# One VectorE product of 2048 columns for two units of a selective scan, in place of two of 1024

## The chip, the cores and the metric

The kernel runs on one core of a Trainium2 chip. The metric is the device time of one execution in microseconds (us), as the median of several runs. Before the change it is 11,066.46 us (three runs, 11,062.12 to 11,069.53). Lower is better. The engines of a core are named as the profile names them: PE (TensorE, matrix products), DVE (VectorE), ACT (ScalarE), POOL (GpSimd) and SP (SyncE, whose queue issues the transfers here). PSUM is the memory that PE writes, eight banks of 512 fp32 columns on each of 128 partitions; the large on-chip memory is SBUF.

## The reference, cut to what matters

The input is eight images of 96 channels and 64 x 64 pixels. The first layer normalizes them, runs a VSS block (a state space block with a two-dimensional selective scan) and a convolutional block with channel attention; the second layer is a linear attention and a feed-forward net in low precision. Nearly all of the time goes into the selective scan:

```python
def selective_scan(xs, dts, A, Bs, Cs, Ds, dt_bias):
    delta = jax.nn.softplus(dts + dt_bias[None, :, :, None])
    ...
    def step(h, inp):
        u_t, d_t, b_t, c_t = inp
        dA = jnp.exp(d_t[..., None] * A)
        h = dA * h + (d_t * u_t)[..., None] * b_t[:, :, None, :]
        y = jnp.einsum('bkdn,bkn->bkd', h, c_t)
        return (h, y)
```

It runs over 4096 pixels, in 4 directions k, for 192 inner channels d with 16 states n each, for each image. For every (image, direction, channel, state) there is a recurrence h = dA * h + (delta * u) * B along the pixels, with B and C depending on direction, state and pixel but not on the channel. The output y is the sum over the 16 states of h * C.

## The kernel before, in words

**Tiling.** Images go in pairs p (four of them), directions k, chunks ci of 1024 pixels (CH), and three tiles T of 128 channels of a pair (192 channels of two images make 384 rows). A *job* is (p, k, ci, T), 192 jobs in all. A job has 16 *units* (j, q): j picks 32 of the tile's 128 channels, q picks 4 of the 16 states, so a unit is 32 x 4 = 128 rows on the partitions and 1024 pixels along the free dimension. Four units with the same j are a *group* g. There are 3072 units, and they are worked off two at a time: 1536 rounds.

**What a unit does.** `fetch` (L1290) loads delta of a group, each channel repeated for four states, into `dl`; `decay` (L1304) makes dA = exp(A * delta) on ACT into `da` (four buffers). `spread` (L1299) has PE copy delta * u of a group, each channel for four states, into the PSUM tile `pu` (1024 columns, two banks) with two matmuls; all four units of the group read it. `weights` (L1268) loads four rows of B (i = 0, tile `bm`) or of C (i = 1, tile `cm`), repeated 32 times over the partitions, 512 KB each; a tile serves all units with the same job triple, batch and q, so there are 512 loads of each kind. `bm` has four buffers, `cm` five.

**The round.** `scan(u)` (L1311) does two units. On DVE it makes the two products pu * B into the two PSUM tiles `pb0` and `pb1` (L1316, L1317), and then the two recurrences with `tensor_tensor_scan` (L1318 to L1324), which read `da` and `pb` and write `hc` (eight buffers); for the later chunks they start from the column `carry`. On POOL it saves the last column as the next `carry` and multiplies `hc` by C (L1326 to L1331). `total` (L1349) then has PE sum the states of a group in PSUM tile `yp`, 16 matmuls, and ACT copies the sum out. For directions 2 and 3 the scan runs backwards over the columns (step -1).

**The order.** All engines of this part are wrapped in `InOrder` (L254), which keeps each engine's instructions in the order of the Python program; this is why most records of the profile carry L266. The main loop (L1400 to L1446) goes through the rounds: it runs one step of the background work, then `scan(u)`, then issues the B loads for units u+4 and u+5 (L1432), the C loads for u+2 and u+3, the decays of u+2 and u+3, and after a group's second round the `spread` of the next group and the `total` of the one before. The background work (convolutions, projections, gates, normalizations of other image pairs) is handed out step by step by the class `Slots` (L283) and runs mainly on PE, ACT and POOL. Waits between engines are semaphores. So are waits of one engine's instruction for another one of the same engine, where the second reads or overwrites what the first wrote or read. An instruction carries one wait itself; further waits stand in separate semaphore instructions ahead of it in the engine's queue, which can hold two each.

**PSUM.** `yp` and `pg` take one bank each, `pu` two, `pb0` and `pb1` two each: eight.

After the loop a tail of some 340 us finishes the last pair (normalizations, attention, feed-forward); ahead of it phase_a prepares the first pair in some 215 us.

Of the kernel before, what the change touches and what calls it, by code (L numbers as in the profile page):

```python
# [9 lines left out]
F32 = mybir.dt.float32  # L10
# [17 lines left out]
CH = 1024  # L28
# [322 lines left out]
def phase_b(  # L351
# [8 lines left out]
    with ExitStack() as ctx:  # L360
# [57 lines left out]
        for i in range(2):  # L418

            t = cp.tile([C + 1, 512], F32, name=f"tn{i}")  # L420
# [3 lines left out]
        bcp = inner.enter_context(tc.tile_pool(name="b_bc", bufs=4))  # L424
# [3 lines left out]
        psc = inner.enter_context(tc.tile_pool(name="b_ps", bufs=1, space=PSUM))  # L428
# [5 lines left out]
        yps = psc.tile([128, 512], F32, name="yp")  # L434
        bank0 = psc.tile([128, 512], F32, name="pg")
        pu = psc.tile([128, CH], F32, name="pu")
        pbs = [psc.tile([128, CH], F32, name=f"pb{i}") for i in range(2)]
        pe = InOrder(tc, nc.tensor, mybir.EngineType.PE)
        ve = InOrder(tc, nc.vector, mybir.EngineType.DVE)
        se = InOrder(tc, nc.scalar, mybir.EngineType.Activation)  # L440
# [6 lines left out]
            for ci in range(NCH) for T in (0, 2, 1)  # L447
        ]
        units = [(job, j, q) for job in range(len(jobs)) for j in range(4) for q in range(4)]
        carries, bcs, dus, dls, sts, das, hcs, prevs, yet = ({} for _ in range(9))  # L450
        turned, resting, squeezed_at = set(), set(), set()

        def where(job):
            p, k, ci, T = jobs[job]
            c = NCH - 1 - ci if k >= 2 else ci
            return p, k, ci, c, T, slice(c * CH, c * CH + CH)

        def batch(u):
            job, j, q = units[u]
            T = jobs[job][3]  # L460
            return j // 2 if T == 2 else T
# [806 lines left out]
        def weights(u, i):  # L1268

            if u >= len(units):  # L1270
                return
            job, j, q = units[u]
            p, k, ci, c, T, at = where(job)
            b = batch(u)
            if (job // 3, b, q, i) in bcs:
                return
            t = bcp.tile([128, CH], F32, name=("bm", "cm")[i], bufs=(4, 5)[i])
            r0 = 32 * (k // 2) + 16 * i + 4 * q
            nc.sync.dma_start(
                t, xd_d[k % 2][2 * p + b][r0 : r0 + 4, at].unsqueeze(0).to_broadcast([32, 4, CH])  # L1280
            )
            bcs[job // 3, b, q, i] = t

# [27 lines left out]
        def scan(u):  # L1311

            job, j, q = units[u]
            p, k, ci, c, T, at = where(job)
            step, last = (-1, 0) if k >= 2 else (1, CH - 1)
            for i in range(2):  # L1316
                ve.tensor_mul(pbs[i], pu, bcs[job // 3, batch(u), q + i, 0])  # L1317
            for i in range(2):  # L1318
                t = hp.tile([128, CH], F32, name="hc")
                carry = carries[p, k][:, T, 4 * j + q + i : 4 * j + q + i + 1]  # L1320
                ve.tensor_tensor_scan(
                    t[:, ::step], das.pop(u + i)[:, ::step], (pbs[i])[:, ::step],
                    0.0 if ci == 0 else carry, ALU.mult, ALU.add,
                )  # L1324
                hcs[u + i] = t
            for i in range(2):  # L1326
                v = u + i
                carry = carries[p, k][:, T, 4 * j + q + i : 4 * j + q + i + 1]
                if ci < NCH - 1:
                    ge.tensor_copy(carry, hcs[v][:, last : last + 1])  # L1330
                ge.tensor_mul(hcs[v], hcs[v], bcs[job // 3, batch(u), q + i, 1])  # L1331
# [61 lines left out]
        for u in range(4):  # L1393
            weights(u, 0)
        for u in range(2):
            weights(u, 1)
# [3 lines left out]
        for u in range(0, n, 2):  # L1400
            g, q = divmod(u, 4)
            if q == 0:
                if g % 4 == 0:
                    job = g // 4 + 1
                    assert slots.first is None
                    p, k, ci, T = jobs[g // 4]
# [15 lines left out]
                    if job < len(jobs):  # L1422
                        p, k, ci, c, T, at = where(job)
# [4 lines left out]
            elif g + 2 < n // 4:  # L1428
                fetch(g + 2)
            slots.run()  # L1430
            scan(u)
            for v in range(u + 4, u + 6):  # L1432
                weights(v, 0)
# [35 lines left out]
        p = NP - 1  # L1469
# [336 lines left out]
def block(tc, a, out):  # L1806
    with tc.tile_pool(name="dram", bufs=1, space=DRAM) as dp:
# [29 lines left out]
        with tc.tile_pool(name="p_const", bufs=1) as pp:  # L1837
            phase_b(
                tc, a, pp, xi_d, xd_d, dl_d, ya_d, ys_d, y_d, zs_d, inp_d, x1_d, ua_d, u_d, g_d,
                cb_d, tn_d, out,  # L1840
            )
# [105 lines left out]
```

## Time and profile before

| | before |
|---|---|
| median of three runs | 11,066.46 us |
| lowest and highest | 11,062.12 and 11,069.53 us |
| span of the profiled execution, first to last instruction | 11,058.4 us |
| mean granted TensorE clock in it | 0.815 |
| DVE's first product of the loop starts | 214.6 us into the span |
| last scan starts | 10,721.3 us |
| products pb on DVE | 3072, 1197 / 1220 / 1251 ns (least, median, most) |
| scans with a carry | 2304, 2310 / 2335 / 2366 ns |
| scans without one | 768, 2254 / 2275 / 2307 ns |
| POOL product hc by cm | 3072, mean 2359 ns |
| ACT decay da | 3072, mean 1140 ns |
| PE spread into pu | 3072 matmuls, mean 944 ns |
| HBM traffic over the span | 165 GB/s |

The profile is one execution taken by the hardware profiler; its span leaves out what lies around the program, so it is put beside the median and not in its place. A group's line reads: line, engine, operation, tile written and tiles read, shapes, number; then the summed busy time and the mean of one; then the idle time of the engine just before them and what ended most of it. The profile counts an instruction from its start to its end, and neighbours on one engine can overlap, so lengths may add up to more than the time that passes. A timeline line reads: start in us, length of the merged group, engine, line, operation, tiles, shapes, number, and in brackets the idle time before it with its releaser, if over 0.15 us. Semaphore instructions are not shown there and not counted as busy.

### The profile page before, as it was taken

To read this page: it belongs to the slowest core of one execution; us is meant where nothing else is said; L and a number is where in the kernel's file an instruction comes from. 1 tells how busy PE (TensorE), PEld (TensorE's weight loads), DVE (VectorE), ACT (ScalarE), POOL (GpSimd) and SP (SyncE) were. 2 spreads that over 40 slices of the span, in tenths; PEclk is the share of its full clock that TensorE was granted. 3 is DMA by queue.
4 is the path that set the end of the run, shared out by engine and by line. 5 is a ranking of instruction groups with operands and counts; after the bars stand their busy time and mean duration, and the time that the engine had idled before them with its cause. 6 is when DMAs were issued, how large, how long until landed. Compare 5 with 4: busy or idle time off the path is not lost.

```text
span 11058.4 us, 128094 instructions
## 1 busy us (share of the span) xinstructions
PE 7887.2 (71%) x39468; PEld 3111.6 (28%) x39468; DVE 10525.7 (95%) x6651; ACT 6596.3 (60%) x9175; POOL 9028.7 (82%) x6649
## 2 busy tenths in 40 slices
PE   7755778655568887767777787776767776665778
PEld 3322333222223332223222332223322222222223
DVE  4999999999999999999999999999999999999974
ACT  2544765544567666556776656565776656665554
POOL 2788877787898888998888887899889888988860
PEclk8877888877788888878878888887878877777889
DMA  3445554454555555666545555566544555644551
GB/s 117 151 165 180 160 156 157 141 188 156 163 185 172 171 172 157 211 214 195 158 152 160 157 178 159 177 220 209 172 157 159 160 164 179 197 157 140 173 157 37
DMA packets 900188, 1834.20 MB, mean 166 GB/s; under 512 B 247965, under 2 KB 421214, under 8 KB 892462
## 3 DMA queue, kind: packets, MB, share of 16 engines
q1 hardware_dynamic: 899502, 1826.01, 52.8%
q8 instruction: 314, 5.14, 0.2%
q14 instruction: 372, 3.05, 0.1%
HBM read 1405.13 MB, written 420.42 MB: 165 GB/s over the span
## 4 chain that ended last, share of the span: by engine, by line
PE 32%; issue 29%; DVE 17%; POOL 11%; ACT 6%; DMA 4%; SPq 0%; DVEq 0%; POOLq 0%; ACTq 0%
PE pu L266 12%; PE yp L266 11%; DVE hc L266 11%; POOL hc L266 7%; PE pg L266 6%; DVE pb L266 5%; ACT u L266 2%; ACT da L266 2%; POOL u L266 2%; PE t L266 2%; PE ps L197 1%; DMA bm<-xd 1%; POOL turn L266 1%; POOL carry L266 1%; ACT L266 1%
## 5 line engine op out<-in xcount | busy, mean ns | idle before, releaser
L266 POOL TENSOR_TENSOR hc<-hc,cm 128x1024 f32<-128x1024 f32 x3072 | 7230.0, 2359 | 591.0 <-DVE hc L266 382.6
L266 DVE TENSOR_TENSOR_SCAN hc<-da,carry,pb 128x1024 f32<-128x1024 f32 x2304 | 5276.8, 2334 | 38.1 <-ACT da L266 31.5
L266 PE MATMUL pu<-du,c_sel 128*128 128x512 f32 x3072 | 2452.5, 944 | 2244.1 <-DVE pb L266 2239.6
L266 DVE TENSOR_TENSOR pb<-pu,bm 128x1024 f32<-128x1024 f32 x3072 | 3601.6, 1220 | 133.9 <-PE pu L266 105.9
L266 ACT ACTIVATE da<-dl,c_alog 128x1024 f32<-128x1024 f32 x3072 | 3352.8, 1140 | 91.4 <-DVE hc L266 73.8
L266 PEld LDWEIGHTS pu<-du,c_sel 128*128 128x128 f32 x3072 | 790.0, 281 | 3521.1 <-DVE pb L266 2784.8
L266 DVE TENSOR_TENSOR_SCAN hc<-da,pb 128x1024 f32<-128x1024 f32 x768 | 1713.1, 2275 | 38.9 <-ACT da L266 22.8
L266 ACT COPY y<-yp 128x256 f32<-128x256 f32 x768 | 284.4, 370 | 2348.9 <-PE yp L266 2198.4
L266 PE MATMUL yp<-hc,c_add 128*32 128x256 f32 x24576 | 1660.8, 416 | 22.6 <-ACT s L266 6.6
L266 PEld LDWEIGHTS yp<-hc,c_add 128*32 128x32 f32 x24576 | 768.6, 120 | 1200.1 <-issue 628.4
L266 POOL COPY carry<-hc 128x1 f32<-128x1 f32 x2304 | 422.5, 183 | 766.1 <-DVE hc L266 744.9
L266 ACT ACT_TABLE_LOAD x566 | 726.2, 1283 | 38.2 <-DMA cb<-zs 16.9
L266 ACT COPY u<-pg 128x512 f32<-128x512 f32 (+6 forms) x397 | 218.3, 550 | 712.3 <-PE pg L266 641.2
L266 POOL TENSOR_TENSOR u<-u,u 96x512 f32<-96x512 f32 (+1 forms) x426 | 537.5, 1269 | 105.9 <-ACT u L266 101.8
L266 POOL TENSOR_TENSOR du<-du,dls 128x1024 f32<-128x1024 f32 x192 | 452.7, 2358 | 91.5 <-ACT dls L266 91.1
L266 ACT COPY u<-yp 96x512 f32<-96x512 f32 (+6 forms) x347 | 188.0, 542 | 465.5 <-PE yp L266 404.5
L266 PE MATMUL pg<-ain,wmain 96*128 96x512 f32 x792 | 354.1, 599 | 0.0
L266 PE MATMUL pg<-ain,wmix 96*128 96x512 f32 x792 | 353.0, 598 | 0.0
L266 PE MATMUL yp<-prev,ident 128*128 128x256 f32 x768 | 321.9, 512 | 39.0 <-ACT u L266 27.4
L266 PEld LDWEIGHTS yp<-prev,ident 128*128 128x128 f32 x768 | 214.5, 283 | 381.8 <-issue 264.3
L266 PE MATMUL pg<-st,dtw 12*128 12x512 f32 x384 | 218.5, 649 | 49.4 <-ACT u L266 28.8
L266 PE MATMUL yp<-st,dtw 12*128 12x512 f32 x384 | 227.9, 674 | 18.3 <-ACT u L266 10.9
(340 smaller groups left out, 7030.2 us busy)
## 6 DMA issues: line engine op xcount, KB each, us to landing
dl<-dl SPq DMA_DIRECT2D x768, 512.0 KB
bm<-xd SPq DMA_DIRECT2D x512, 512.0 KB
cm<-xd SPq DMA_DIRECT2D x512, 512.0 KB
du<-xi SPq DMA_DIRECT2D x192, 512.0 KB
dl<-dls SPq DMA_DIRECT2D x192, 512.0 KB
ya<-y SPq DMA_DIRECT2D x384, 128.0 KB
prev<-ya SPq DMA_DIRECT2D x384, 128.0 KB
xi<-u SPq DMA_DIRECT2D x152, 256.0 KB
```

The source lines that it names most:

```text
L197: nc.tensor.matmul(bank[r, :].rearrange("p (h w) -> p h w", w=W), w[:, t if len(which) > 1 or w is wmix else 0, columns], pads[b][:, 8 * j ...
L266: op(*args, **kw)
```

## The change

The two PSUM tiles `pb0` and `pb1` become one tile `pb` of 2 x 1024 columns (the same four banks). The B loads of two units (q even and q odd) go into the two halves of one SBUF tile `bm` of 2 x 1024 columns, with two buffers in place of four of half the size; the tile is taken when the even half is loaded. In `scan`, one `tensor_mul` of 2 x 1024 columns replaces the two of 1024: `pu` is read twice through a dimension of stride 0, `bm` whole, and `pb` is written whole. The two scans read a half of `pb` each. C loads, scans, POOL, PE and ACT work and the loop stay as they are.

```diff
-        pbs = [psc.tile([128, CH], F32, name=f"pb{i}") for i in range(2)]
+        pb = psc.tile([128, 2, CH], F32, name="pb")
...
-            t = bcp.tile([128, CH], F32, name=("bm", "cm")[i], bufs=(4, 5)[i])
+            if i:
+                t = to = bcp.tile([128, CH], F32, name="cm", bufs=5)
+            else:
+                if q % 2 == 0:
+                    pairs[job // 3, b, q] = bcp.tile([128, 2, CH], F32, name="bm", bufs=2)
+                t = pairs[job // 3, b, q - q % 2]
+                to = t[:, q % 2, :]
             r0 = 32 * (k // 2) + 16 * i + 4 * q
             nc.sync.dma_start(
-                t, xd_d[k % 2][2 * p + b][r0 : r0 + 4, at].unsqueeze(0).to_broadcast([32, 4, CH])
+                to, xd_d[k % 2][2 * p + b][r0 : r0 + 4, at].unsqueeze(0).to_broadcast([32, 4, CH])
             )
             bcs[job // 3, b, q, i] = t
...
-            for i in range(2):
-                ve.tensor_mul(pbs[i], pu, bcs[job // 3, batch(u), q + i, 0])
+            ve.tensor_mul(
+                pb, pu.unsqueeze(1).to_broadcast([128, 2, CH]), bcs[job // 3, batch(u), q, 0]
+            )
             for i in range(2):
                 t = hp.tile([128, CH], F32, name="hc")
                 carry = carries[p, k][:, T, 4 * j + q + i : 4 * j + q + i + 1]
                 ve.tensor_tensor_scan(
-                    t[:, ::step], das.pop(u + i)[:, ::step], (pbs[i])[:, ::step],
+                    t[:, ::step], das.pop(u + i)[:, ::step], pb[:, i, ::step],
                     0.0 if ci == 0 else carry, ALU.mult, ALU.add,
                 )
                 hcs[u + i] = t
```

More of the change, by code (lines that the diff above doesn't have):

```diff
@@ L449, in phase_b @@
         units = [(job, j, q) for job in range(len(jobs)) for j in range(4) for q in range(4)]
-        carries, bcs, dus, dls, sts, das, hcs, prevs, yet = ({} for _ in range(9))
+        carries, bcs, pairs, dus, dls, sts, das, hcs, prevs, yet = ({} for _ in range(10))
         turned, resting, squeezed_at = set(), set(), set()
```

## The prediction

> **What bounds the kernel now.** I read the busy times first, then the slices, then VectorE's groups, then the timeline of a stretch in the middle.
>
> ```profile
> PE 7887.2 (71%) x39468; PEld 3111.6 (28%) x39468; DVE 10525.7 (95%) x6651; ACT 6596.3 (60%) x9175; POOL 9028.7 (82%) x6649
> ...
> DVE  4999999999999999999999999999999999999974
> ```
>
> VectorE (DVE) is busy for 95% of the span and at 90% or more in every slice but the first and the last two. POOL follows with 82%. So the time between about 215 us and 10,724 us, the scan loop, is VectorE's own stream of instructions, and what lengthens or shortens that stream moves the end by as much.
>
> ```profile
> L266 DVE TENSOR_TENSOR_SCAN hc<-da,carry,pb 128x1024 f32<-128x1024 f32 x2304 | 5276.8, 2334 | 38.1 <-ACT da L266 31.5
> ...
> L266 DVE TENSOR_TENSOR pb<-pu,bm 128x1024 f32<-128x1024 f32 x3072 | 3601.6, 1220 | 133.9 <-PE pu L266 105.9
> ```
>
> The loop is 1536 rounds of two products (pb) and two scans (hc). Other engines hold VectorE up very little: 134 us in front of products, 77 us in front of the two kinds of scans (38.1 here, 38.9 in the group without a carry), 211 us in all. The next view, a timeline of VectorE, tells what a round takes (start, length of the merged group, instructions in it):
>
> ```profile
> 5001.25 2.34 DVE L266 TENSOR_TENSOR pb<-pu,bm 128x1024 f32<-128x1024 f32 x2
> 5003.50 4.57 DVE L266 TENSOR_TENSOR_SCAN hc<-da,carry,pb 128x1024 f32<-128x1024 f32 x2
> 5007.99 2.34 DVE L266 TENSOR_TENSOR pb<-pu,bm 128x1024 f32<-128x1024 f32 x2
> ```
>
> Two products of 1.22 us make 2.34 us and not 2.44: neighbours overlap. The next group starts before the last ends: 5001.25 + 2.34 = 5003.59, against 5003.50. In the trace's instruction records the medians from start to start are product to product 1.115 us, product to scan 1.130, scan to scan 2.254, scan to product 2.238. A round is their sum, 6.737 us (5007.99 - 5001.25 = 6.74). Every instruction starts some 0.09 us before the one ahead has ended, so the recorded lengths overstate what an instruction costs. **This overlap is what the change puts at stake.**
>
> **Who waits for whom.** In the built program before, each product and scan waits for VectorE's own semaphore, but always for the instruction before the last one: order P0 P1 S0 S1, where S0 needs P0, S1 needs P1, the next P0 overwrites what S0 read, the next P1 what S1 read. One instruction always lies between, so that wait has long been met. In the program after, the order is P S0 S1. S0 needs P, the instruction directly ahead; the next P overwrites both halves of pb, so it waits for S1, directly ahead too. Only S1 keeps a free start. All 1536 S0 and nearly all P have such a wait.
>
> **What a wait for the instruction directly ahead costs.** The loop of before has none, but the tail after it has some 75, on VectorE too:
>
> ```profile
> 10778.22 1.54 DVE L266 SCALAR_TENSOR_TENSOR tn<-tn,c_on,cb 128x512 f32<-128x512 f32 x2 [2.17 <-ACT cb L266]
> ```
>
> Two instructions of 752 ns each in one buffer, the second reading the first: 1.54 us is 2 x 0.752 + 0.035. No overlap, and a gap of 34 to 36 ns from end to start; 48 casts behind a TENSOR_SCALAR show the same. That is the price where the waiting instruction itself carries the wait. Where an instruction has more waits than it can carry, the others stand in a separate semaphore instruction ahead of it, and this costs more:
>
> ```profile
> 10803.93 0.75 DVE L266 SCALAR_TENSOR_TENSOR w_dt.float<-t,c_vec,w_dt.float 96x512 f32<-96x512 f32 x1 [8.99 <-ACT w_dt.float L266]
> 10804.78 2.44 DVE L266 TENSOR_SCALAR up<-w_dt.float,c_vec 96x512 f32<-96x512 f32 x1
> ...
> 10809.96 0.75 DVE L266 SCALAR_TENSOR_TENSOR w_dt.float<-t,c_vec,w_dt.float 96x512 f32<-96x512 f32 x1 [1.49 <-ACT w_dt.float L266]
> 10810.74 0.48 DVE L266 TENSOR_SCALAR up<-w_dt.float,c_vec 96x512 f32<-96x512 f32 x1
> ```
>
> The first pair goes through such a semaphore instruction: 10804.78 - 10803.93 - 0.747 = 0.107 us of gap. The second pair waits directly: 10810.74 - 10809.96 - 0.747 = 0.036 us. A semaphore instruction with two waits is recorded at 50 ns instead of 21, so with the late wait listed first I take 0.107 + 0.029 = 0.136 us.
>
> **The sum for a round.**
> - The joint product: a product of 512 columns (tn) takes 684 ns, of 1024 columns 1220, so 536 ns for 512 columns, and 1220 + 2 x 536 = 2292 ns for 2048. [...]
> - P to S0: S0's wait for P stands in a semaphore instruction with two waits (P first, then ScalarE): 0.136. From P's start to S0's start 2.292 + 0.136 = 2.428, against 1.115 + 1.130 = 2.245 now: **+0.183**.
> - S0 to S1: free as before, 2.254: 0.
> - S1 to the next P: S1 takes 2.324. Half of the products (those behind no new pu) carry the wait themselves, 0.035; the other half, which also wait for PE's new pu, have it in a semaphore instruction, 0.107; mean 0.071. So 2.395 against 2.238: **+0.157**.
>
> Together +0.340 us a round, x 1536 = **+522 us**. The rounds without a carry (a quarter) have start to start times 60 ns shorter before and after; the difference is the same.
>
> Off this I take: S0 now starts on a drained engine, and a scan behind a scan is 16 ns shorter from start to start than one behind a product (2.238 against 2.254): -25 us. The same for the joint product (a product behind a scan is recorded at 1209, one behind a product at 1224; 11 ns below my 1220): -17 us. And some of the 211 us that VectorE now idles for others goes: a round is 5% longer for PE, ScalarE and the loads alike, and where VectorE waits for another engine its own gap is hidden. Bounds 0 and 100 us; I take 30, since 115 such stops of 0.1 to 0.2 us hidden are about 17 and the rest is catching up. Sum 522 - 25 - 17 - 30 = **+450 us**.
>
> **What lies beside it and costs nothing.** The B loads keep their place in SP's queue and their number (512); two buffers of two units hold what four of one did. The first load of a pair may now be issued only when the joint product is done, about 1.1 us later than now, and the joint product needs the second half 1.1 us earlier; the loads are issued two rounds (13 us) ahead. The view of pb shows how close this is now:
>
> ```profile
>   PE pu L266: 105.9, 45
>   ACT da L266: 54.3, 43
>   DMA bm<-xd: 25.3, 19
> ```
>
> Only 19 products waited for a load, 25 us in all. The cover is the two rounds, which grow by 0.68 us. If the cover were gone, each of the 256 first uses of a pair would lose up to 1.1 us, 282 us; I take 0. PE's spread into pu is released by the end of a round's last product and needed by the next round's first, two scans later; that window grows from 4.40 us (1.130 - 1.220 + 2.254 + 2.238) to 4.82 (0.136 + 2.254 + 2.324 + 0.107). PSUM stays at eight banks. POOL and ScalarE get the same work at a slower pace.
>
> [...] The row: dependent neighbours stand 0.035 to 0.107 us apart, free ones overlap by 0.09. [...]
>
> **The rivals.**
> - *The waits cost nothing (faster).* If S0 could start on P's tail as now, P to S0 would be 1.115 + 2 x 0.536 = 2.187 (free start), against 2.245: -0.058 x 1536 = -89 us, **10,977**. The change stops being slower where the two gaps, 0.207 us together in my sum, have become an overlap of 0.133 (0.207 - 0.340); none of the tail's dependent pairs starts before the one ahead has ended. 4%: 3% faster, 1% where gain and loss cancel.
> - *Only one of the two holds costs, or each only the direct 35 ns.* P to S0 alone: 0.183 x 1536 = +281; both at 35 ns: (2.327 - 2.245) + (2.359 - 2.238) = 0.203, +312. Less the same 72 us of relief: **about 11,290**. Against it: the built program has both waits, and in which place. 6%.
> - *The loads become late.* Forecast plus up to 282 us: **11,600 to 11,800**. Against it the 25 us above. 7%.
> - *The change isn't in the program.* The built program has 1536 products of 2048 columns instead of 3072 of 1024. 0%.
>
> **How the numbers follow.** The profiled execution spans 11,058.4 us; the median of three runs is 11,066.46, 8 us more, which I keep: 11,066 + 450 = **11,516**. Forecast 83%. Lower end: hold of 0.107 instead of 0.136 (-45) and 100 us of idle time back instead of 30 (-70): 11,400. Upper end: none of the 72 us of relief and some 20 us of late loads: 11,610. Measurement can tell about 0.2% (22 us) from no change. Faster 3%, same 1%, slower 96%.
>
> **What would show it.** After the change: 1536 products of about 2.28 us; start to start about 2.42 us from product to scan, scan to scan still 2.25, scan to product 2.36 or 2.43 in turn; VectorE's busy time falls, since the overlap is no longer counted twice, while the span grows. I am wrong if the scan's start overlaps the product's end, or if the waits for bm grow past 100 us.

## The result and the profile after

The changed kernel takes **11,511.7 us** (median of four runs, 11,505.08 to 11,519.01) against 11,067.99 for the kernel before beside it (four runs). The ratio is 1.040, with a 95% interval of 1.0387 to 1.0414: **slower by 4%**, 444 us. The forecast was 11,516 us. The profiled execution spans 11,514.0 us, 455.6 more than that of before. The 12 us between 444 and 455.6 are a matter of which execution was profiled: that of before spans 10 us less than the median of its kernel, that of after 2 us more.

The page of after, busy times, VectorE's row of slices, and its three large groups:

```profile
PE 7973.9 (69%) x39468; PEld 3138.2 (27%) x39468; DVE 10735.8 (93%) x5115; ACT 6605.7 (57%) x9175; POOL 9032.1 (78%) x6649
...
DVE  4999999999999999999999999999999999999974
...
L266 DVE TENSOR_TENSOR_SCAN hc<-da,carry,pb 128x1024 f32<-128x1024 f32 x2304 | 5281.5, 2334 | 168.5 <-ACT da L266 13.0
...
L266 DVE TENSOR_TENSOR pb<-pu,bm 128x2048 f32<-128x2048 f32 x1536 | 3532.2, 2300 | 200.3 <-PE pu L266 71.5
...
L266 DVE TENSOR_TENSOR_SCAN hc<-da,pb 128x1024 f32<-128x1024 f32 x768 | 1714.4, 2274 | 79.9 <-PE yp L266 14.2
```

VectorE still bounds the kernel: 90% or more in every slice but the first and the last two. It issues 1536 instructions fewer, and the joint product of 2300 ns is shorter than two of 1220. So by recorded lengths the change is a gain of 140 ns a round. The loss is in two places. VectorE's busy time rose by 210 us, because neighbours that overlapped no longer do. The rest stands in the last column: the idle time ahead of scans and products has gone from 211 us to 449 (168.5 + 200.3 + 79.9), and the releasers named explain only a part of it. In front of the carry scans, ACT's decay accounts for 13.0 of 168.5 us. The rest is spread over 1152 scans, the first of each round with a carry, as gaps too short to be listed. In the trace's records of the loop, gaps of up to 0.15 us add up to 299 us after and to 1 us before; longer ones fell from 189 us to 129. Idle time without a releaser, in many small equal pieces, is what a wait for the same engine's own previous instruction looks like here.

The timeline of after, VectorE (start, length of the merged group, number):

```profile
5299.24 4.59 DVE L266 TENSOR_TENSOR_SCAN hc<-da,carry,pb 128x1024 f32<-128x1024 f32 x2
5303.86 2.30 DVE L266 TENSOR_TENSOR pb<-pu,bm 128x2048 f32<-128x2048 f32 x1
5306.30 4.58 DVE L266 TENSOR_TENSOR_SCAN hc<-da,carry,pb 128x1024 f32<-128x1024 f32 x2
5310.98 2.30 DVE L266 TENSOR_TENSOR pb<-pu,bm 128x2048 f32<-128x2048 f32 x1
5313.41 4.58 DVE L266 TENSOR_TENSOR_SCAN hc<-da,carry,pb 128x1024 f32<-128x1024 f32 x2
```

Add start and length and compare with the next start. 5303.86 + 2.30 = 5306.16, and the scan starts at 5306.30: a gap of 0.13 us (0.14 with these rounded figures). 5306.30 + 4.58 = 5310.88, and the product starts at 5310.98: 0.10. 5299.24 + 4.59 = 5303.83, next start 5303.86: 0.03. Before, each of these sums lay *past* the next start by 0.09. Nothing is named as a releaser, because no other engine is late.

The views by tile, of after, show the waits for other engines in front of the joint product and its scans (us, times):

```profile
  PE pu L266: 71.5, 28
  ACT da L266: 25.8, 17
  DMA bm<-xd: 22.3, 9
```

All three are smaller than before (105.9, 54.3, 25.3): a slower VectorE gives everybody else more time. That holds for PE too, though its granted clock was 0.803 against 0.815 and its spread took 968 ns against 944. The loads, which now come in pairs, didn't become late.

### The profile page after: what moved, and what is told of

Same layout as the page of the kernel before. It is cut to its first block, busy times and chain, and to the rows that moved or that the text cites. A ratio compares the mean times of both kernels' runs of the same rounds, so it can differ in the third digit from the quotient of the medians.

```text
span 11514.0 us, 124663 instructions
## 1 busy us (share of the span) xinstructions
PE 7973.9 (69%) x39468; PEld 3138.2 (27%) x39468; DVE 10735.8 (93%) x5115; ACT 6605.7 (57%) x9175; POOL 9032.1 (78%) x6649
## 5 line engine op out<-in xcount | busy, mean ns | idle before, releaser
L266 DVE TENSOR_TENSOR_SCAN hc<-da,carry,pb 128x1024 f32<-128x1024 f32 x2304 | 5281.5, 2334 | 168.5 <-ACT da L266 13.0
L266 PE MATMUL pu<-du,c_sel 128*128 128x512 f32 x3072 | 2519.7, 968 | 2691.7 <-DVE pb L266 2687.2
L266 DVE TENSOR_TENSOR pb<-pu,bm 128x2048 f32<-128x2048 f32 x1536 | 3532.2, 2300 | 200.3 <-PE pu L266 71.5
L266 DVE TENSOR_TENSOR_SCAN hc<-da,pb 128x1024 f32<-128x1024 f32 x768 | 1714.4, 2274 | 79.9 <-PE yp L266 14.2
L266 ACT ACT_TABLE_LOAD x566 | 726.2, 1283 | 37.7 <-DMA cb<-zs 18.1
```

What stands on the lines that cost most here:

```text
L266: op(*args, **kw)
```

## The experiments

The question is which part of the change costs the 444 us. My theory: the two holds, that is, S0 and P now waiting for the instruction directly ahead of them on their own engine. Rivals: the joint tiles by themselves (four banks, paired loads), the instruction of 2048 columns by itself, and late loads. None of the runs leaves out work of the reference. Times of the kernel before beside them lie between 11,069 and 11,075 us. S to P and the like below are medians from start to start, in us, in rounds with a carry where nothing from another engine is late.

| run | time, us | ratio to before (95%) |
|---|---|---|
| joint tiles, two products | 11,777.4 | 1.0641 (1.0625 to 1.0656) |
| paired loads alone | 11,078.2 | 1.0007 (0.9998 to 1.0016) |
| product and scan in turn | 12,814.5 | 1.1578 (1.1561 to 1.1595) |
| in turn in half of the rounds | 11,415.1 | 1.0308 (1.0293 to 1.0322) |
| touch ahead | 11,739.8 | 1.0607 (1.0591 to 1.0623) |
| products in SBUF | 15,808.8 | 1.4283 (1.4259 to 1.4307) |
| places swapped | 11,095.9 | 1.0025 (1.0014 to 1.0035) |
| one hold gone | 11,299.4 | 1.0207 (1.0192 to 1.0223) |
| product a round ahead | 11,522.4 | 1.0410 (1.0394 to 1.0425) |
| the same, phase moved | 11,461.2 | 1.0348 (1.0334 to 1.0362) |
| sums and loads earlier | 12,074.3 | 1.0910 (1.0895 to 1.0925) |
| decays split | 12,276.3 | 1.1091 (1.1075 to 1.1106) |

**The joint tiles, with two products of 1024 columns** (from after):

```diff
-            ve.tensor_mul(
-                pb, pu.unsqueeze(1).to_broadcast([128, 2, CH]), bcs[job // 3, batch(u), q, 0]
-            )
+            for i in range(2):
+                ve.tensor_mul(pb[:, i, :], pu, bcs[job // 3, batch(u), q, 0][:, i, :])
```

> Both tiles joined as in the change (bm of two units, pb of two halves), but two products of 1024 columns again, each on its half. My theory: each wait is again for the instruction before the last one, so a round is 6.737 us and the time that of before, 11,066 us (11,040 to 11,095). Rival, the joined tiles cost the time (loads of a pair that must both have landed, buffers freed two units at a time): it stays near 11,510 us.

Measured 11,777.4: a miss, and the expectation was badly thought out. In the built program waits go by tile, not by half: P1 waits for P0 because both write pb, S0 waits for P1, the next P0 for S1. That is three holds in place of none. The timeline of this run:

```profile
5303.20 2.50 DVE L266 TENSOR_TENSOR pb<-pu,bm 128x1024 f32<-128x1024 f32 x2
5305.84 4.58 DVE L266 TENSOR_TENSOR_SCAN hc<-da,carry,pb 128x1024 f32<-128x1024 f32 x2
```

Two products take 2.50 instead of 2.34: P0 to P1 is 1.267 (a gap of 0.035) where it was 1.115, and P1 to S0 is 1.365 (a gap of 0.133) where it was 1.130. So the run says nothing about the tiles alone. It shows two other things: a hold costs the same with narrow products, and where the tile is joint anyway, the joint *instruction* is the better one, by 266 us (11,777.4 - 11,511.7).

**The paired loads alone** (from before: the joint `bm` tile, everything else as it was; its last changed line is):

```diff
-                ve.tensor_mul(pbs[i], pu, bcs[job // 3, batch(u), q + i, 0])
+                ve.tensor_mul(pbs[i], pu, bcs[job // 3, batch(u), q, 0][:, i, :])
```

> Only the B loads go into a joint tile of two units (two buffers), as in the change; pb stays two tiles and the products stay two of 1024 columns. Unlike in the run with both tiles joined, no instruction now waits for the one directly ahead. My theory: the time of before, 11,066 us (11,040 to 11,095). Rival, loads that must land in pairs and buffers freed in pairs cost part of the 445 us: over 11,150 us, with more waits of products for bm than the 25 us of before.

Measured 11,078.2, ratio 1.0007, and 27.9 us of waits for bm: no cost. Loads and the `bm` tile are out.

**Product and scan in turn** (from before; order P0 S0 P1 S1, so that each scan directly follows its product, and no instruction is wider):

```diff
                 ve.tensor_mul(pbs[i], pu, bcs[job // 3, batch(u), q + i, 0])
-            for i in range(2):
                 t = hp.tile([128, CH], F32, name="hc")
```

> The kernel before with another order on VectorE: product, scan, product, scan; no joint product and no joint tile. Each scan now reads what the instruction directly ahead wrote; no product overwrites what the instruction directly ahead read. My theory: two holds of 0.133 us and two lost overlaps, product to scan 1.220 + 0.133 = 1.353 us, scan to product 2.238 as before, a round 2 x (1.353 + 2.238) = 7.182 us, +0.445 x 1536 = +683 us, less up to 130 us of idle time that comes back: 11,620 to 11,750 us. Rival, the width of the joint instruction costs the time: 11,066 us, as the instructions are the same as before.

Measured 12,814.5: the undisturbed round is 2 x (1.339 + 2.264) = 7.206, as expected (a hold of 0.13 between product and scan, with narrow products in tiles of their own), but 1,000 us more came from somewhere else:

```profile
L266 DVE TENSOR_TENSOR pb<-pu,bm 128x1024 f32<-128x1024 f32 x3072 | 3723.9, 1212 | 889.0 <-PE pu L266 867.2
```

The group of products waits 867 us for PE's spread, and the two groups of scans wait another 262 us for PE's sums in yp. In this order the last product that reads pu stands one scan later, so PE has the time of one scan to fill pu again instead of two. That was still an argument until the next run.

**In turn only in rounds behind which pu is not refilled** (from before; P0 S0 P1 S1 for q = 0, P0 P1 S0 S1 for q = 2):

```diff
-                ve.tensor_mul(pbs[i], pu, bcs[job // 3, batch(u), q + i, 0])
-            for i in range(2):
+                if i == 0 or q == 0:
+                    ve.tensor_mul(pbs[i], pu, bcs[job // 3, batch(u), q + i, 0])
+                if i == 0 and q == 2:
+                    ve.tensor_mul(pbs[1], pu, bcs[job // 3, batch(u), q + 1, 0])
```

> The kernel before with the order product, scan, product, scan only in the first round of each group; in the second round, whose last product frees pu for PE, both products come first as before. This tells why the order in turn in every round cost 1745 us where I had expected 550 to 680. My theory: the surplus was PE, which there had one scan's time to refill pu and here has two again; so only the holds of half the rounds are left, 0.47 us x 768 = +360 us less up to 100 us of stalls that come back: 11,290 to 11,430 us, and products wait for pu some 100 us in place of 867. Rival, the order in turn costs its surplus in every round: half of 1745, about 11,940 us.

Measured 11,415.1. With pu's window left as it was, the waits for pu are 79.9 us instead of 867.2, and the loss is the holds': 768 x 0.469 (7.206 - 6.737) = 360 us by this, and some 341 found (11,415.1 less 11,415.1 / 1.0308). The gap of a held scan is the 0.133 us of the changed kernel here too, with narrow products and another order.

**Touch ahead** (from after; a copy of one column of da into the first scan's `hc` buffer ahead of the product, so that the waits for ACT and for the buffer are met there and S0 has only the wait for P):

```diff
+            ts = [hp.tile([128, CH], F32, name="hc") for i in range(2)]
+            ve.tensor_copy(ts[0][:, 0:1], das[u][:, 0:1])
...
-                t = hp.tile([128, CH], F32, name="hc")
+                t = ts[i]
```

> The changed kernel with one more VectorE instruction a round, ahead of the joint product: a copy of one column of da into the buffer that the first scan will write whole. It takes the first scan's waits for ScalarE, PE and POOL, so that the scan carries its wait for the product itself, without semaphore instructions ahead. My theory: product to scan falls from 2.432 to 2.335 us (gap 0.035 in place of 0.133), and the copy itself lies in the gap between the second scan and the product; scan to product about 2.36 in place of 2.39. A round 6.96 in place of 7.08 us, -195 us, less up to 60 us that comes back as stalls: 11,310 to 11,380 us. Rival, the hold costs the same wherever the wait stands: the copy's 0.06 us a round comes on top, 11,510 to 11,610 us.

The hold shrank as expected: P to S0 is 2.334, a gap of 0.035 instead of 0.133. The time, 11,739.8, missed:

```profile
L266 DVE COPY hc<-da 128x1 f32<-128x1 f32 x1536 | 214.4, 140 | 515.7 <-PE yp L266 351.6 <-ACT da L266 53.0 <-POOL carry L266 38.6
```

The small copy needs its `hc` buffer one joint product earlier than the scan does, and waits 516 us, most of it for PE, which reads `hc` last. Here the wait that was met earlier was met more often.

**Products in SBUF** (from before; products go into `hc` buffers and the scans run in place there, so that no pb tile is written twice):

```diff
-        pbs = [psc.tile([128, CH], F32, name=f"pb{i}") for i in range(2)]
...
+            pbs = [hp.tile([128, CH], F32, name="hc") for i in range(2)]
...
-                t = hp.tile([128, CH], F32, name="hc")
+                t = pbs[i]
```

> The kernel before with the products written into the SBUF buffers hc that the scans then overwrite in place; two products of 1024 columns, order and waits as before. It is the reference for the next two kernels. Theory: neither a product to SBUF nor a scan with two SBUF inputs takes longer, 11,066 us (11,040 to 11,100). Rival: two SBUF inputs on VectorE collide with POOL's products, scans of over 2.4 us and 11,150 us or more.

Measured 15,808.8. Three groups of its page:

```profile
L266 POOL TENSOR_TENSOR hc<-hc,cm 128x1024 f32<-128x1024 f32 x3072 | 9735.5, 3174 | 702.0 <-DVE hc L266 480.0
L266 DVE TENSOR_TENSOR_SCAN hc<-da,carry,hc 128x1024 f32<-128x1024 f32 x2304 | 7397.4, 3249 | 719.0 <-ACT da L266 719.0
...
L266 POOL COPY carry<-hc 128x1 f32<-128x1 f32 x2304 | 2489.9, 1081 | 48.3 <-DVE hc L266 48.3
```

The scans now read both inputs from SBUF. They take 3249 ns on average instead of 2334, POOL's products 3174 instead of 2359, and POOL's one-column copies 1081 instead of 183. These means mix two kinds of instruction, as a stretch of the timeline shows:

```profile
5002.56 0.18 POOL L266 COPY carry<-hc 128x1 f32<-128x1 f32 x1
5002.82 2.36 POOL L266 TENSOR_TENSOR hc<-hc,cm 128x1024 f32<-128x1024 f32 x1
...
5004.86 4.65 DVE L266 TENSOR_TENSOR_SCAN hc<-da,hc 128x1024 f32<-128x1024 f32 x2 [3.52 <-ACT da L266]
5005.12 2.18 POOL L266 COPY carry<-hc 128x1 f32<-128x1 f32 x1
...
5007.38 4.26 POOL L266 TENSOR_TENSOR hc<-hc,cm 128x1024 f32<-128x1024 f32 x1
```

A copy takes 0.18 us or 2.18, a product 2.36 or 4.26. In the records 1264 of the 2304 copies take under 0.2 us and nearly all others 2.1 to 2.2, and 1770 of the 3072 products under 2.4 us and the others 3.8 to 4.4. Of the 2304 scans with a carry 1017 still take under 2.4 us, though all of them run in place, so running in place isn't what slows the others. With both scan inputs in SBUF the kernel takes 15,808.8 us, so in the next ones one input stays in PSUM.

**Places swapped** (from before: da into PSUM, the products into SBUF; the order unchanged):

```diff
-        pbs = [psc.tile([128, CH], F32, name=f"pb{i}") for i in range(2)]
+        pbs = [gp.tile([128, CH], F32, name=f"pb{i}") for i in range(2)]
...
-            das[u] = wp.tile([128, CH], F32, name="da", bufs=4)
+            das[u] = psc.tile([128, CH], F32, name="da", bufs=2)
```

> The kernel before with the places of the scan's two inputs swapped: da in PSUM (two buffers in place of four), pb0 and pb1 in SBUF. The scan still has one input in each memory, so it should not meet POOL as the run with both inputs in SBUF did. Order and waits on VectorE as before. It is the reference for the next two. Theory: scans of 2.33 us, a round of 6.74 us, 11,066 to 11,200 us, where the upper end is for ACT that has only two buffers of da. Rival: what made the scans slow was pb in SBUF itself, scans of 3 us and over 15,000 us.

Measured 11,095.9, ratio 1.0025: a round of 6.745 us and scans of 2329 ns. With one input in each memory, the scan does not slow down. This makes room to take a hold away without taking a wait away: pb in SBUF can have two buffers.

**One hold gone** (from after, with the swap, and the joint `pb` in two buffers; the next product no longer overwrites what S1 has just read, while S0 still needs P):

```diff
-        pb = psc.tile([128, 2, CH], F32, name="pb")
...
-            das[u] = wp.tile([128, CH], F32, name="da", bufs=4)
+            das[u] = psc.tile([128, CH], F32, name="da", bufs=2)
...
+            pb = gp.tile([128, 2, CH], F32, name="pb", bufs=2)
```

> The changed kernel with the places swapped (da in PSUM, two buffers; pb of two units in SBUF) and two buffers of the joint pb. The product no longer overwrites what the scan directly ahead reads; the first scan still reads what the product directly ahead wrote. My theory: scan to product is free again, 2.24 us in place of 2.39; product to scan stays 2.43; a round 6.93 us, 0.20 more than the reference with swapped places: 300 us above it less up to 80 us of stalls that come back, so 11,280 to 11,370 us if that is at 11,066. Rival, only the total of work counts and the joint product itself is what costs: as the changed kernel, 440 us above the reference.

Measured 11,299.4, in the expected range. Its timeline:

```profile
5009.16 2.27 DVE L266 TENSOR_TENSOR pb<-pu,bm 128x2048 f32<-128x2048 f32 x1
5011.56 4.47 DVE L266 TENSOR_TENSOR_SCAN hc<-da,pb 128x1024 f32<-128x1024 f32 x2
```

The gap between product and scan is still there: 5009.16 + 2.27 = 5011.43, next start 5011.56. In the records S1 to P is 2.242, free again (2.238 before), and P to S0 is 2.396 (a gap of 0.132). So 212 us (11,511.7 - 11,299.4) went, but not all by the hold: S1 to P is 0.146 us shorter (224 us in 1536 rounds), the product into SBUF is 0.035 us shorter (54 us), and the places swapped alone cost 27 us in their own run; the rest came back as waits for others. Against that run (11,095.9) the kernel with one hold is 203 us slower, where the two holds cost 444.

**The product a round ahead** (from the kernel just shown; `product(u)` is its `tensor_mul`, and the next round's stands between the two scans, so that no instruction needs the one directly ahead):

```diff
+                if i == 0 and u + 2 < len(units):
+                    product(u + 2)
...
+            if q == 0 and g + 1 < n // 4:
+                spread(g + 1)
             if q == 2:
-                if g + 1 < n // 4:
-                    spread(g + 1)
```

> As the kernel with one hold gone, and the joint product of the next round is put between the two scans of a round; the spread into pu is issued a round earlier, so that PE keeps two scans of time for it. Every wait of VectorE for itself is now for the instruction before the last one or older. My theory: product to scan 2.19, scan to scan's successor 2.24 to 2.26, a round 6.68 us, 0.055 less than before: 85 us below the reference with swapped places, 10,980 us (10,950 to 11,030) if that is at 11,066. Rival, a joint product costs time of its own beyond its columns: at or above the reference.

```profile
5000.69 2.27 DVE L266 TENSOR_TENSOR pb<-pu,bm 128x2048 f32<-128x2048 f32 x1
5002.87 4.58 DVE L266 TENSOR_TENSOR_SCAN hc<-da,carry,pb 128x1024 f32<-128x1024 f32 x2
5007.37 2.27 DVE L266 TENSOR_TENSOR pb<-pu,bm 128x2048 f32<-128x2048 f32 x1
```

This timeline shows the change from the other side. 5000.69 + 2.27 = 5002.96, and the scan starts at 5002.87: the overlap is back. 5007.37 - 5000.69 = 6.68, against 6.74 before the change. In the records P to S is 2.182, S to P 2.242, S to S 2.257, together 6.681. **In rounds that nothing disturbs, a joint product that holds nobody is worth 0.056 us, some 86 us in 1536 rounds; with both holds a joint product costs 0.347.** (Against the run with the places swapped, 6.745 us a round, it is 0.064.) But the time, 11,522.4, missed the expected one widely. It lies where the rival had it (a joint product costs time of its own), but the rows above refute that, and the loop waits 702 us for others.

```profile
L266 DVE TENSOR_TENSOR_SCAN hc<-da,carry,pb 128x1024 f32<-128x1024 f32 x2304 | 5320.0, 2335 | 390.2 <-ACT da L266 216.5 <-PE yp L266 85.6 <-POOL du L266 66.9
```

The scans wait for ACT's decays, PE's sums and POOL.

Three more runs tried to clear these waits by order alone. **Phase moved** starts the background work two steps later (from the kernel just shown):

```diff
-        slots.at = 0
+        slots.at = 2
```

> The kernel with the product a round ahead, and the counter by which the background work is planned starts two steps later, so that long pieces of PE work begin right behind the spread into pu again and not ahead of it. In the run without this the rounds that nothing disturbed took the 6.68 us of my theory, but VectorE idled 679 us in front of products and scans in place of 211. My theory: PE's place in its queue made ScalarE, and by it da, late; with the phase moved the idle time falls to 220 to 350 us, and the time to 10,990 to 11,130 us. Rival, two buffers of da are too few for this order: it stays over 11,400 us.

Measured 11,461.2: the waits for POOL's du fell from 94 us to 5, but those for da were still 283 (314 before this edit), and those for yp came to 172 and for bm to 122. **Sums and loads earlier** brings `total` into a group's first round and loads B two units sooner (from the one with the phase moved; the fetch of `prev` for the sums moves with it):

```diff
-            for v in range(u + 4, u + 6):
+            for v in range(u + 6, u + 8):
                 weights(v, 0)
...
-            if q == 0 and g + 1 < n // 4:
-                spread(g + 1)
-            if q == 2:
+            if q == 0:
+                if g + 1 < n // 4:
+                    spread(g + 1)
```

> The kernel with the product a round ahead and the phase moved; besides, the sums over the states (total) go to the end of a group's first round, next to the spread, and the B loads are issued one round earlier. With the product a round ahead a group's first scan follows the scan ahead of it at once, so the buffer that it writes, which total must have read, is needed one product's time earlier, and each B load too. Idle time in the run with the phase moved: ACT da 290 us, PE yp 172, bm 122, of 648. My theory: the waits for yp and bm go, and most of those for da, which come from ScalarE waiting for yp in its queue; idle time 200 to 330 us and 10,980 to 11,110 us, level with before or a little below. Rival, two buffers of da hold ScalarE back in this order: waits for da stay near 290 us, 11,200 us or more.

Measured 12,074.3. The loads were cured (bm 18 us) and the wait for yp went, but da waits rose:

```profile
L266 DVE TENSOR_TENSOR_SCAN hc<-da,carry,pb 128x1024 f32<-128x1024 f32 x2304 | 5328.5, 2336 | 932.7 <-ACT da L266 906.0 <-POOL hc L266 17.4 <-POOL carry L266 3.8
```

The decays were held up in ACT's own queue, behind the copies out of yp. The group of these copies, in the run with the phase moved and then in this one:

```profile
L266 ACT COPY y<-yp 128x256 f32<-128x256 f32 x768 | 280.9, 366 | 184.6 <-PE yp L266 166.3 <-issue 5.0 <-DMA prev<-ya 5.0
```
```profile
L266 ACT COPY y<-yp 128x256 f32<-128x256 f32 x768 | 286.0, 372 | 2010.0 <-PE yp L266 1847.7 <-DMA dl<-dl 62.1 <-DMA prev<-ya 39.2
```

They wait 1848 us for PE's sums instead of 166, as they now come to the head of the queue before the sums are made, and the next decay stands behind them. **Decays split** puts the two decays of a round on both sides of one background step, with the loads earlier and `total` at the start of a group's second round:

```diff
+            if q == 2 and g > 0:
+                total(g - 1)
...
-            for v in range(u + 2, min(u + 4, n)):
-                decay(v)
+            if u + 2 < n:
+                decay(u + 2)
...
+            if u + 2 < n:
+                decay(u + 3)
```

> The kernel with the product a round ahead and the phase moved, with the B loads one round earlier, the sums over the states at the start of a group's second round in place of its end, and ScalarE's two decays of a round put around one step of background work in place of one behind the other. Reason: with the product a round ahead, da is needed one product's time (2.2 us) sooner behind the scan that frees its buffer, so ScalarE had some 4 us for background work between two pairs of decays in place of 6.6. My theory: the stalls of the last kernels are the order of ScalarE's and PE's queues and not the joint product; undisturbed rounds stay at 6.68 us, idle time in front of VectorE's loop falls from 648 us to 200 to 400, and the time to 10,990 to 11,250 us. Rival, with two buffers of da any order of this kind stalls: over 11,400 us.

Measured 12,276.3, with 1132 us of waits for da (883.8 + 248.2 us in the two groups of scans). The copies out of yp still wait 1134 us for PE, and ACT now loads a function table 948 times instead of 566, at 1283 ns each: 382 more, 490 us of ACT's time, in an order in which the decays no longer stand side by side. Undisturbed rounds still take 2.182 + 2.242 + 2.257. So the shorter round is there in the versions without holds, but none of them is faster than the kernel before: the gain was seen in rounds and never in a time. The last three runs all landed in the range of their rival, that two buffers of da are too few. **What stays open:** whether these waits come from da having two buffers in PSUM instead of four in SBUF, or from the order of ACT's and PE's queues. Two buffers alone are not enough to explain them, since with the places swapped and the old order the loss is 0.25%. Four da buffers in PSUM beside pu, yp and pg would make twelve banks, where the tiles of the kernel before make eight, and that was not tried; a narrower pb was not tried either.

## Why the prediction was right, step by step

| step, us a round | predicted | measured |
|---|---|---|
| P to S0 (hold through a semaphore instruction) | +0.183 | +0.188 |
| S0 to S1 | 0 | +0.009 |
| S1 to the next P (hold, half of it direct) | +0.157 | +0.150 |
| sum | +0.340 | +0.347 |
| x 1536, us | +522 | +533 |
| relief by a drained engine, us | -42 | none (contained in the rows above) |
| idle time back, us | -30 | -85 |
| tail, us | 0 | +8 |
| total against the profiled span, us | +450 | +456 |

- **The holds** carry the result and are shown, not only argued: put holds into the kernel before, in half of its rounds, and they cost some 341 us, for 360 by the rows; take one away by a second buffer and its 0.146 us a round go; take both away and the round is shorter than before. The prices of gap held to within 0.003 us: direct 0.035 (predicted 0.035), through a semaphore instruction 0.104 (0.107), with two waits 0.133 (0.136). The first two came from the tail of the kernel before, from instructions of other shapes and other operations; the third was an estimate from the second and the recorded lengths of semaphore instructions. (The prediction's two subtractions give 0.103 and 0.033 with the rounded starts that it prints; the records have the 0.107 and 0.036.) Of the products behind a scan, 768 carry the wait themselves and 761 have it in a semaphore instruction (634 of them with one wait, 127 with a load's wait as well, gap 0.090), which is the half and half of the prediction.
- **The joint product** was put at 2292 ns by extending the rows of 512 and 1024 columns, and takes 2300. That reading pu twice with stride 0 costs nothing no run shows by itself; against this extension it costs at most these 8 ns.
- **The relief by a drained engine** failed. I took 16 ns off S0 to S1 and 11 ns off the product because instructions behind a longer neighbour were recorded a little shorter. S0 to S1 became 9 ns longer instead, and the product took 2300 ns and not 2281. In the records, held instructions are the longest: a held scan takes 2347 ns, a free one 2340 behind a product and 2324 behind a scan, and a held product of 1024 columns 1232 (joint tiles, two products) against 1224 and 1209. 42 us of the sum were wrong.
- **The idle time back** was mis-sized the other way: loop 10,956.5 us against 10,509.0 is +447.5, so 533 - 447.5 = 85 us came back, against 30 taken and bounds of 0 to 100. Waits of 211 us shrank to some 140 (449 less the holds' own gaps, 1536 x (0.133 + 0.068) = 309). The two slips of 42 and 55 us leave 13 us, and these and the 12 us between spans and medians stand against 11 us more for the holds (533 for 522) and the tail's 8. So that only 4 us lie between forecast and median is in part luck. The tail's 8 us have no cause in the change that is known: in the traces of the other runs, with the same tail, it lasts 336 to 344 us, against 335 before and 343 after.
- **VectorE's busy time** was said to fall, and it rose by 210 us. The overlapped time was counted once already before: 3601.6 us for 3072 products is 1172 ns each, not 1220. What had been overlap of two instructions is now time of one alone. Of the loop's 447.5 us, 238 are more idle time (449 - 211) and 210 are this. Only the share fell, from 95% to 93%, as the gaps are idle.
- **The cover of the loads** held: 22.3 us of waits, and paired loads alone are worth 1.0007.
- **The rivals.** That waits cost nothing is refuted by the gaps. Its arithmetic was nevertheless right: 2.187 for a free P to S0 was computed, and 2.182 is found where nothing holds (with the product in SBUF). That only one hold costs, 11,290, describes the kernel with one hold gone (11,299.4), not this one. Late loads didn't come.

**What decided.** The gaps of 0.035, 0.104 and 0.133 us against an overlap of 0.09: with them a round became 0.347 us longer, and without holds one instruction fewer made it 0.056 us shorter.

## What to carry to other kernels

On an engine that bounds the kernel, look at start to start times and not at recorded lengths: free neighbours overlap here by 0.09 us, and an instruction that needs the one directly ahead of it loses this and 0.035 to 0.133 us more, so here joining two instructions shortened a round only where an unrelated instruction still stood between the joint one and those that need its result or free its buffer. Read the waits in the built program before and after, since they go by tile: two halves of one tile hold each other up although they share no element (two products into the halves of pb start 1.267 us apart, into two tiles 1.115). When an instruction is moved ahead to hide a hold, every buffer and input that it touches is needed that much earlier, and this can cost more than the hold: the touch ahead took 0.098 us a round off the gap in front of the scan, 151 us in 1536 rounds, and its copy waited 516 us.

## What the runs showed of the hardware

- **Four gaps for one kind of wait.** A wait for the instruction directly ahead leaves a gap of 0.035 us where the instruction carries the wait itself (the same between two products, from a scan to a product, and from a product to a scan), 0.104 us in a semaphore instruction with one wait, and 0.133 us in one with two waits and the late one first; where the late one stood second, 0.090. The 0.133 was seen from product to scan and the 0.090 from scan to product, so that the order of the waits makes the difference is likely but not tested by itself.
- **Two SBUF inputs on VectorE beside POOL.** A scan with both inputs in SBUF went from 2334 to 3249 ns, and POOL's product from 2359 to 3174; with one input in PSUM the scan takes 2334 (pb there, kernels before and after) or 2329 to 2337 (da there, places swapped and one hold gone). The one-column copies took 0.18 us, or about 2.18, nearly a scan's length. In the stretch shown the long one, from 5005.12 to 5007.30, ends with the first of the two scans, which the records have from 5004.86 to 5007.33. What in the memory or between the engines makes it so, no run shows.
- **Where the product goes.** The product of 2048 columns takes 2300 ns into PSUM (changed kernel) and 2265 into SBUF (one hold gone).
